# Layer 0 of a four-layer graph network: per-node weights generated on TensorE, 128 nodes at a time, and applied to all eight batches

## The chip, the cores and the metric

The kernel runs on one core of one Trainium2 chip. The time is the device time of one execution in microseconds (us), and lower is better. One core has TensorE for matmuls (PE, with PEld for its weight loads), VectorE (DVE), ScalarE (ACT), GpSimd (POOL) and SyncE (SP, here only a queue that issues transfers). Sixteen DMA engines move the data. PE writes to PSUM, eight banks of 512 f32 values in each of 128 partitions, and DVE or ACT carry the results from there to SBUF.

## What is computed

The input x is 8 batches x 2048 nodes x 64 features in f32, adj is a 2048 x 2048 adjacency matrix whose rows are normalised. Four layers follow each other; each takes the layer norm and relu of x as h, and adds to x what its layer makes of h. The change is in layer 0:

```python
w = jnp.einsum('nd,dkio->nkio', embedding, weight)   # N=2048, D=16, K=3, 64 -> 64
b = jnp.einsum('nd,do->no', embedding, bias)
As = [eye(N), A, 2.0 * (A @ A) - eye(N)]
x_g = jnp.einsum('knm,bmc->bnkc', stack(As), x)      # x is h here
out = jnp.einsum('bnki,nkio->bno', x_g, w) + b
```

So each node has three 64 x 64 weight matrices of its own, a mix of 16 shared ones with the node's embedding as coefficients. Layer 1 takes three steps of adjacency product, two small maps and a relu. Layer 2 is one adjacency product and a map, layer 3 comes down to a sum over all nodes.

## The kernel before, in words

The 8 batches go as 4 pairs p; a pair fills 128 feature rows (2 x 64). The 2048 nodes are 4 blocks nb of 512 columns and 16 chunks m of 128 rows. BT (L94) holds the sign pattern of the adjacency matrix, [128, 16 chunks, 2048], 128 KB in each partition for the whole run; the row scales come back through crow (`load_crow`, L199), a row that is broadcast by a DMA, when a product leaves PSUM (`scaled`, L288). An operand of a product is held as two rounded parts H and L (`halves`, L275), so one block of a product is 32 matmuls 128 x 128 x 512 (`chunks`, L303). A product of all nodes is 4 such blocks.

Layer 0 needs, per pair, t1 = A h and t2 = A t1. The t1 products of pairs 0 and 1 are made in the prologue while the adjacency rows arrive (L593 to L656). The main loop (L858 to L960) then goes pair by pair: for pairs 2 and 3 the four blocks of t1 (`term1`, L488), then for each block its t2 (L923) and `node_weights` (L814). That function makes, for 128 nodes t and 8 embedding indices dg, all 8 mixes' outputs at once on PE: 6 f32 matmuls (3 terms x 2 batches, each on its own half of the array's rows, L828) into the PSUM tile y. DVE then multiplies each of the 8 blocks of 64 columns by that node's embedding value and adds it to x, one scalar_tensor_tensor each (L837). A block of 512 nodes is 48 of these matmuls and 64 of these DVE instructions. Behind each block come layer 1's norm and the storing of x (`keep`, L806).

The first term t0 is h turned to feature rows: `store_planes` (L167) splits h into 16-bit planes and stores them, `load_planes` (L182) reads them back with two transposing DMAs on SP, `join_planes` (L193) puts them together on ACT. `split_next` (L178) and `go_on` (L254) are called between pieces of work and take the next such step, or the next stage of a norm (`norm_stages`, L220). `make_weights` (L689) prepares the small matrices of the later layers. Layer 1's operands are made by `begin_next` (L772) and `first_operand` (L788); its step is `step1` (L1017).

Each engine takes its instructions in a fixed order. The order is settled when the program is built, from the order of the code, the buffers that are free and the `issue_after` marks, so a transfer can stand earlier in its queue than its line suggests, but never goes round another one at run time. MD is a copy of BT's pattern in DRAM in bf16, stored one chunk per block (L951) and read by layer 1's tests of the input (`test_load`, L975).

## Time and profile before

| what | value |
|---|---|
| median of 3 runs | 1176.61 us (1176.37 to 1176.89) |
| the profiled execution | 1180.88 us, of which its span is 1179.2 us |
| PE busy | 1157.1 us (98%) |
| DVE, ACT, POOL busy | 745.2, 293.9, 243.6 us |
| end of the prologue's last product, start of layer 0's main part | 79.15 us |
| first product of layer 1 | 609.44 us |
| DMA | 147 MB, mean 125 GB/s |

A line of a view of groups reads: source line, engine, operation, output <- inputs by the program's names, shapes, count | busy us, mean ns of one | idle time of the engine just before them. The chain of waits is followed back from the last instruction; each piece has its start, its length and what it is. An f32 matmul leaves two records in these views, so `x96` are 48 matmuls; a matmul on the rounded parts leaves one.

### The profile page before, as it was taken

The numbers are of one execution on the slowest core, as the hardware profiler recorded it, in microseconds if no ns is written. First come the engines' busy times: TensorE is split into PE (matmuls) and PEld (weight loads), VectorE is DVE, ScalarE is ACT, GpSimd is POOL, SyncE is SP. The second block draws the span as 40 slices with busy tenths as digits, with TensorE's granted clock in tenths as the row PEclk, the third lists the DMA queues.
The fourth block names the chain that finished last, engine by engine and source line by source line (L and its number), as shares of the span: only waits on it lengthen the run. The fifth ranks groups of instructions, "written<-read, shape, count | busy, mean of one in ns | idle before, by whom it ended". The sixth has DMA issues, their size and how long they took to land.

```text
span 1179.2 us, 19459 instructions
## 1 busy us (share of the span) xinstructions
PE 1157.1 (98%) x7614; PEld 802.6 (68%) x7614; DVE 745.2 (63%) x1933; ACT 293.9 (25%) x465; POOL 243.6 (21%) x259
## 2 busy tenths in 40 slices
PE   9999999999999999999999999999999999999995
PEld 7775555555575556755557777777777777787884
DVE  5557888777847777277775436545643755565674
ACT  5721222111121111111122343334323433211110
POOL 5611332211132111011110004002300410241121
PEclk9999999999999999999999999999999999999998
DMA  9973554323342234222219534663853464441432
GB/s 351 401 191 86 152 151 124 107 74 81 80 140 81 72 84 97 69 56 70 67 54 206 126 82 135 149 137 100 187 118 95 131 160 104 130 152 59 138 114 75
DMA packets 131478, 147.02 MB, mean 125 GB/s; under 512 B 77512, under 2 KB 90312, under 8 KB 129328
## 3 DMA queue, kind: packets, MB, share of 16 engines
q1 hardware_dynamic: 114496, 86.25, 28.8%
q0 software_dynamic: 13456, 53.66, 14.9%
q10 hardware_dynamic: 3424, 5.77, 1.5%
q8 instruction: 62, 1.02, 0.4%
q14 instruction: 40, 0.33, 0.1%
HBM read 88.74 MB, written 39.59 MB: 109 GB/s over the span
## 4 chain that ended last, share of the span: by engine, by line
PE 79%; DVE 7%; DMA 6%; issue 4%; POOL 2%; ACT 1%; POOLq 0%; ACTq 0%; DVEq 0%; SPq 0%
PE bv L306 32%; PE y L828 26%; PE bv_2b L306 3%; PE bv_1b L306 3%; PE bv_3b L306 3%; PE bv_0b L306 2%; PE bn L753 2%; PE ph L1028 2%; DMA acc<-xs 2%; DVE z L227 2%; DMA xs<-acc 2%; POOL rstd L240 1%; DMA BT<-in_adj_dram 1%; PE bv_2a L554 1%; PE bv_1a L554 1%
## 5 line engine op out<-in xcount | busy, mean ns | idle before, releaser
L306 PE MATMUL bv<-BT,H 128*128 128x512 f32 x768 | 302.8, 394 | 0.0
L306 PE MATMUL bv<-BT,L 128*128 128x512 f32 x768 | 299.2, 390 | 0.0
L837 DVE SCALAR_TENSOR_TENSOR acc<-y,emb,acc 128x128 f32<-128x128 f32 x512 | 175.9, 344 | 57.1 <-PE y L828 57.1
L306 PEld LDWEIGHTS bv<-BT,H 128*128 128x128 f32 x768 | 144.1, 188 | 37.2 <-PE bn L753 6.5
L306 PEld LDWEIGHTS bv<-BT,L 128*128 128x128 f32 x768 | 144.2, 188 | 29.2
L837 DVE SCALAR_TENSOR_TENSOR odd<-y,emb,odd 128x128 f32<-128x128 f32 x448 | 153.1, 342 | 0.0
L240 POOL TENSOR_TENSOR rstd<-var,mhalf 128x8 f32<-128x8 f32 x64 | 106.3, 1663 | 173.4 <-DVE var L237 173.0
L828 PE MATMUL y<-wt,t0T 64*128 64x512 f32 x512 | 137.9, 607 | 2.6 <-DVE odd L837 1.6
L306 PE MATMUL bv<-BT,L_u 128*128 128x512 f32 x256 | 101.7, 397 | 3.7 <-DVE L_u L283 3.7
L306 PE MATMUL bv<-BT,H_u 128*128 128x512 f32 x256 | 101.7, 397 | 0.4 <-DVE L_u L283 0.4
L291 DVE TENSOR_TENSOR g<-bv,crow 128x512 f32<-128x512 f32 x48 | 33.1, 689 | 102.2 <-PE bv L306 102.2
L232 ACT ACTIVATE sq<-z 128x512 f32<-128x512 f32 x64 | 40.4, 632 | 202.3 <-DVE z L227 126.3
L828 PEld LDWEIGHTS y<-wt,t0T 64*128 64x128 f32 x512 | 44.1, 185 | 65.7 <-issue 59.6
L809 POOL TENSOR_TENSOR acc<-acc,wl 128x512 f32<-128x512 f32 x16 | 21.4, 1339 | 314.8 <-DVE z L227 314.1
L809 POOL TENSOR_TENSOR acc<-acc,b2r 128x512 f32<-128x512 f32 x16 | 21.3, 1330 | 252.0 <-DVE z L227 252.0
L828 PE MATMUL y<-wt,t1T 64*128 64x512 f32 x256 | 66.8, 589 | 0.0
L243 DVE SCALAR_TENSOR_TENSOR z<-z,rstd 128x512 f32<-128x512 f32 x64 | 43.5, 685 | 35.5 <-POOL rstd L240 35.5
L306 PEld LDWEIGHTS bv<-BT,L_u 128*128 128x128 f32 x256 | 48.6, 190 | 17.1 <-DVE L_u L283 7.2
L173 ACT COPY pl<-z 128x512 uint16<-128x512 uint16 x48 | 27.3, 616 | 130.4 <-DVE z L243 100.2
L306 PEld LDWEIGHTS bv<-BT,H_u 128*128 128x128 f32 x256 | 48.6, 190 | 14.5 <-PE bn_u L753 2.4
L227 DVE SCALAR_TENSOR_TENSOR z<-mean,acc 128x256 f32<-128x256 f32 x112 | 54.8, 532 | 2.6 <-ACT pl L173 2.1
L1034 ACT COPY g<-ph 64x512 f32<-64x512 f32 x64 | 37.2, 581 | 68.9 <-PE ph L1028 67.8
(228 smaller groups left out, 1789.5 us busy)
## 6 DMA issues: line engine op xcount, KB each, us to landing
BT<-in_adj_dram POOLq DMA_DIRECT2D x16, 1024.0 KB, 12.3
crow<-crowD SPq DMA_DIRECT2D x64, 256.0 KB, 3.3
st<-in_adj_dram SPq DMA_DIRECT2D x64, 256.0 KB, 4.0
xs<-acc POOLq DMA_DIRECT2D x32, 256.0 KB, 2.7
MD<-BT POOLq DMA_DIRECT2D x16, 512.0 KB, 5.0
acc<-xs SPq DMA_DIRECT2D x32, 256.0 KB, 4.4
hp<-pl POOLq DMA_DIRECT2D x31, 256.0 KB, 2.6
acc<-in_x_dram SPq DMA_DIRECT2D x24, 256.0 KB, 4.7
```

The lines of the kernel that those rows point to most:

```text
L173: nc.scalar.copy(pl[:, s], hv[:, s])
L227: firsts.append(nc.vector.scalar_tensor_tensor(split(z)[:, :, e], each(mean)[:, :, e, None].to_broadcast([P, 4, C]), -1.0 / C, nodes(xt)[: ...
L232: squares.append(nc.scalar.activation(sq, z, AF.Square))
L240: powers.append(nc.gpsimd.tensor_tensor(rstd, var, mhalf, op=ALU.pow))
L243: scales.append(nc.vector.scalar_tensor_tensor(groups(h), g, 0.0, rstd[:, :, None].to_broadcast([P, 8, C]), op0=ALU.max, op1=ALU.mult))
L291: ahead.append(nc.vector.tensor_tensor(to, ps.rearrange("p (q t) -> p t q", t=4), crow, op=ALU.mult))
L306: nc.tensor.matmul(ps, hl[m // 4][i][:, m % 4, :], BT[:, m, nb * 512:(nb + 1) * 512], start=(m == 0 and i == 0), stop=(m == NCH - 1 and i ...
L554: last = nc.tensor.matmul(ps, hls[p][m // 4][i][:, m % 4, :], BT[:, m, nb * 512:(nb + 1) * 512], start=(m == 0 and i == 0), stop=(m == NCH ...
L809: nc.gpsimd.tensor_tensor(nodes(acc), nodes(acc), more, op=ALU.add)
L828: nc.tensor.matmul(y[:, bb, :], terms[k][hs_, ts], wt[hs_, k, dg * 512:(dg + 1) * 512], start=(k == 0), stop=(k == K - 1),)
L837: last = nc.vector.scalar_tensor_tensor(xj, yd, ec, old, op0=ALU.mult, op1=ALU.add)
L1034: nc.scalar.copy(gT[nb + i][two[bb], :], ph[bb][two[bb ^ i], :])
```

## The change

All of layer 0's products come first, for all four pairs, and then one stage makes and applies the weights for all eight batches.

**Products.** After the prologue six rounds run, each four blocks of 32 matmuls: t2 of pairs 0 and 1, then t1 and t2 of pair 2 and of pair 3. Each block's result, t1 and t2, is stored to DRAM (TD) by `store_t`, two DMAs on SP with runs of 64 values; t0 takes the same way as soon as it is joined. Behind the first 8 blocks run the norms of pairs 2 and 3, behind the next 8 the planes of pairs 0 and 1; `add_bias` adds the bias to x on POOL and stores it for 16 blocks. MD is stored in the first 16 blocks. `make_emb` turns the embedding so that its 16 values stand in four groups of rows (0, 32, 64, 96), and `make_wg` loads the 16 shared matrices in that layout and combines the terms, which was done in wt before.

**Weights.** Then BT's chunks 4 to 15 are given up: their space takes w1 and w2, two buffers each, 96 KB per partition. For each of 16 groups of 128 nodes, `make_w` in 6 steps makes the weights with small f32 matmuls (16 rows deep, four row groups), evicted by DVE (half of each step) and ACT (the other half), and `apply_w` multiplies each node's three terms of all 8 batches by that node's weights; nodes n and n + 64 of a group go together, the other one's columns being zeros. The steps of group g + 1 lie between the applications of group g. All these matmuls are chained in the written order. Results go to DRAM (yD).

**After it.** `x1_load` and `x1_add` bring a block's result back, add it to x and start layer 1's norm: for pair 0 between the groups, for pairs 1 to 3 in the steps of layer 1 for the pair before. BT's chunks 4 to 15 are read back from MD by 12 DMAs on POOL that widen bf16 to f32, and layer 1's first operands follow.

The core of the diff:

```diff
-    BT = adjp.tile([P, NCH, N], F32R, name="BT")
+    BTs = [(sums_ if g else adjp).tile([P, 4, N], F32R, name=f"BT_{g}") for g in range(NCH // 4)]
...
+    def store_t(k, p, nb, t):
+        for e in range(2):
+            nc.sync.dma_start(
+                TD[nb][k, :, :, :, 2 * p + e, :].rearrange("i t h q -> i (t h) q"),
+                t[e * C:(e + 1) * C, :].rearrange("i (f q) -> i f q", q=C),
+            )
...
-    def node_weights(p, nb, terms, between):
...
-                y = psums[-1].tile([P, 2, 512], F32, tag="big", name=f"y_{p}_{nb}_{t}_{dg}")
...
-                    last = nc.vector.scalar_tensor_tensor(
-                        xj, yd, ec, old, op0=ALU.mult, op1=ALU.add
-                    )
...
+    rounds = [("b", 0), ("b", 1), ("a", 2), ("b", 2), ("a", 3), ("b", 3)]
...
+            fetch_t0()
+            split_next()
+            if i < 8:
+                norm_0(2 + i // 4, nb)
+            elif i < 16:
+                restage(i // 4 - 2, nb)
+                acc = load_x(0, i // 4 - 2, nb)
+                add_bias(acc, i // 4 - 2, nb)
+            elif i < 20:
+                make_emb(nb)
+            elif i < 22:
+                make_wg(i - 20)
...
+            t = product(hl, nb, nm, term(1 if own else 2, f"t{2 - own}T_{nm}"), crow, fill=fill)
+            store_t(1 if own else 2, p, nb, t)
...
+    def make_w(g, i):
...
+        ps = [psy.tile([P, 2, 512], F32, tag="gen", name=f"gen_{g}_{i}_{h}", bufs=3) for h in range(2)]
+        if i < 4:
+            w, per, at = ws_[g][0], 4, 4 * i
+            for o in range(4):
+                for r in range(4):
+                    rs = slice(32 * r, 32 * r + D)
+                    multiply(ps[r // 2][:, r % 2, o * P:(o + 1) * P],
+                             wg[rs, at + o, :P], e[rs, :], start=True, stop=True)
+        else:
+            w, per, at = ws_[g][1], 8, 8 * (i - 4)
+            for o in range(8):
+                for c in range(2):
+                    for r in range(4):
+                        rs = slice(32 * r, 32 * r + D)
+                        multiply(ps[r // 2][two[c], r % 2, o * C:(o + 1) * C],
+                                 wg[rs, at + o, P:], e[rs, two[c]], start=True, stop=True)
+        for h in range(2):
+            to = w.rearrange("p n (r o) -> p r n o", r=4)[:, 2 * h:2 * h + 2, :, at:at + per]
+            src = ps[h].rearrange("p r (o n) -> p r n o", o=per)
+            moved[h] = (nc.vector.tensor_copy, nc.scalar.copy)[h](to, src)
...
+    def apply_w(g, u):
+        bk, s_ = divmod(u, 8)
...
+        for m in range(3):
+            for j in range(4):
+                x_ = 32 * bk + 8 * j + s_
+                lhsT = (
+                    tt.rearrange("p h b q -> p (h b) q")[:, :, x_], tt[:, 1, :, x_], t2[:, :, x_]
+                )[m]
+                rhs = (w1_[:, x_, :], w1_[:, C + x_, :], w2_[:, x_, :])[m]
+                wide = 32 if m == 0 else 2 * B
+                multiply(yps[g, bk][32 * j:32 * j + wide, s_ * C:(s_ + 1) * C], lhsT, rhs,
+                         start=(m == 0), stop=(m == 2))
...
+    load_group(0)
+    for i in range(6):
+        make_w(0, i)
+    for g in range(NCH):
+        if g + 1 < NCH:
+            load_group(g + 1)
+        u = 0
+        for i, count in enumerate((3, 3, 2, 3, 3, 2)):
+            if g + 1 < NCH:
+                make_w(g + 1, i)
+            for _ in range(count):
+                apply_w(g, u)
+                u += 1
...
+        if g % 4 == 3:
+            x1_load(0, g // 4)
...
+    BTs[1:] = [hi2.tile([P, 4, N], F32R, name=f"BTr_{g}") for g in range(1, NCH // 4)]
+    for m in range(4, NCH):
+        nc.gpsimd.dma_start(bt(m), rows_of(MD, m))
...
+    x1_add()
+    all_done()
+    while splits:
+        split_next()
+    for q in range(3):
+        first_operand(q)
+    begin_next(0, 3)
```

## The prediction

> **What bounds the kernel now.** I read the chain of waits first, then its pieces in order of time, then the groups by form, then stretches of time with their DMA load.
>
> ```profile
> PE 79%; DVE 7%; DMA 6%; issue 4%; POOL 2%; ACT 1%; POOLq 0%; ACTq 0%; DVEq 0%; SPq 0%
> PE bv L306 32%; PE y L828 26%; PE bv_2b L306 3%; PE bv_1b L306 3%; PE bv_3b L306 3%; PE bv_0b L306 2%; PE bn L753 2%; PE ph L1028 2%; DMA acc<-xs 2%; DVE z L227 2%; DMA xs<-acc 2%; POOL rstd L240 1%; DMA BT<-in_adj_dram 1%; PE bv_2a L554 1%; PE bv_1a L554 1%
> ```
>
> TensorE sets the time. A quarter of the chain is y, the matmuls that go. The chain's pieces of pair 1 and of a layer-1 step price them:
>
> ```profile
> 234.28 20.99 PE y L828 x96
> 255.26 7.49 PE bv_2b L306 x32
> ...
> 667.42 1.02 PE ph L1028 x8
> 668.43 0.93 PE bn L753 x64
> 669.37 11.10 PE bv L306 x48
> 680.47 1.09 PE bn L753 x64
> ```
>
> A block of 512 nodes is 7.49 us of product and then 20.99 us of y; 48 f32 matmuls, so one per 437 ns, two of them side by side on the array's halves. Small matmuls pack too: bn is 32 f32 matmuls 64 x 64 x 64 in 0.93 us, one per 29 ns, four at a time.
>
> ```profile
> L837 DVE SCALAR_TENSOR_TENSOR acc<-y,emb,acc 128x128 f32<-128x128 f32 x512 | 175.9, 344 | 57.1 <-PE y L828 57.1
> L1041 DVE TENSOR_TENSOR bn<-bn,wl 128x1024 f32<-128x1024 f32 x16 | 19.7, 1230 | 14.0 <-PE bn L753 14.0
> L424 DVE COPY crow<-pt_c 128x512 f32<-128x512 f32 x4 | 2.8, 691 | 2.2 <-PE pt_c L317 2.1
> L281 ACT CAST H_t<-pt_t 128x512 fp32r<-128x512 f32 x16 | 9.3, 583 | 54.3 <-PE pt_t L317 54.3
> ```
>
> DVE's 1024 small adds wait for PE, not the reverse: they go without gain by themselves. The three other rows price an eviction from PSUM: a COPY of 512 costs what other DVE operations of 512 do, so 1024 cost 1.23 us; on ACT about 1.17 us.
>
> ```profile
> 79.20:609.40 530.20, 527.11 (x2395) 305.08 (x2393) 384.89 (x1227) 88.33 (x146) 103.75 (x110) 1.00 0.34 93
> 30.00:60.00 30.00, 29.79 (x127) 23.13 (x126) 16.46 (x44) 21.66 (x26) 19.29 (x22) 1.00 1.07 395
> 58.00:64.00 6.00, 6.00 (x28) 4.50 (x27) 2.94 (x19) 2.01 (x2) 1.13 (x2) 1.00 1.06 216
> 609.00:716.00 107.00, 106.62 (x880) 83.50 (x880) 53.68 (x102) 36.89 (x62) 12.53 (x17) 1.00 0.58 136
> ```
>
> The columns are the stretch, its length, busy time of PE, PEld, DVE, ACT and POOL, granted clock, DMA share, GB/s. Layer 0's main part lasts 530 us with the DMA engines a third busy. Full, they moved 395 GB/s of long rows while the adjacency came in, and 216 GB/s where the shared weights came in runs of 256 bytes (58 to 64 us).
>
> **The change, part by part.** Against the 530 us:
>
> *Removed: y.* 16 blocks x 20.99 = 336 us of PE. The 24 product blocks stay at 7.49 us, so do the transposes of t1.
>
> *Added: generation and application.* Per group of 128 nodes there are 4 steps of 16 generation matmuls (16 rows x 128 columns, 128 moving), 2 steps of 64 (64 columns, 64 moving) and 16 x 12 = 192 application matmuls (32 or 16 columns, 64 moving).
> A matmul of the first kind streams a quarter of y's 512 columns, and four row groups run where y has two: 437/4/2 = 55 ns, or 109 ns if only two run at once. A step is 0.87 us (to 1.75).
> The second kind has the size of bn: 29 ns, or half if eight tiles run at once; a step is 1.86 us (0.93 to 1.86).
> Application goes in four column groups of 64 moving columns: I take bn's 29 ns, 12 of them 0.35 us.
>
> The matmuls alone would be 4 x 0.87 + 2 x 1.86 + 5.6 = 12.8 us per group. But PSUM decides: a step needs two tiles of three. Its second tile is the one that DVE evicts from the step before, and the order is written, so PE stands there. From the end of a step's generation to its next use: about 0.17 us until the last record has drained, 0.07 to DVE, 1.23 copy, 0.05 back: 1.52 us. In this time PE has 2 or 3 applications, 0.70 to 1.04 us, and two changes of tile size. These cost little: 32 bn matmuls at 437/8/2 = 27.3 ns would be 0.87 us, and the chain shows 0.93 to 1.09, so 0.06 to 0.22 us for both.
> So a group is 4 x (0.87 + 1.52) + 2 x (1.86 + 1.52) = 16.3 us; 16 groups, of which the first has no application beside it, and 5.6 us for the last application: **267 us**. Below, if evictions hide behind applications (loop 1.13 us) and eight tiles run at once: 4 x 2.0 + 2 x 2.06 = 12.1, in all 199. Above, with two row groups and an eviction 24% longer, as ACT's scattered 16-bit copies are (765 ns at L196 against 616 at L173): 4 x 3.57 + 2 x 3.68 = 21.6, in all 352. I take the middle: y already runs its row groups side by side, and nothing in the code lets PE round the eviction.
>
> [...]
> [...]
>
> *Moved: the transfers of layer 0, into the product stage.* For blocks 3 to 15 one block carries the x load, h, the kept x, planes out and in, crow, bias and MD (about 2 MB) and two stores of 256 KB in 256-byte runs plus the transposing reads (0.77 MB). At 395 and 216 GB/s that is 5.1 to 6.1 + 3.6 us, so 8.7 to 9.7 us per block where PE needs 7.49 and some 0.4 for transposes. SP issues two transposes and about seven more:
>
> ```profile
> 88.87 2.53 SPq L186 DMA_TRANSPOSE pt<-hp  x2
> ...
> 114.42 0.38 SPq L156 DMA_DIRECT2D acc<-in_x_dram  x1
> ```
>
> That is 5.1 us, under a block. The new wait on SP: `store_t` stands until `scaled` is done, and behind it stand the next x, planes and crow. Cover: crow has two buffers, lands in 3.3 us and is wanted a block later. If the engines stay full the cover is gone, scaled comes late and PE stops at the second PSUM bank. 13 blocks x 0 to 1.8 us is up to 23; with queueing I bound it by 0 and 40 and take **15 us**. Turning the embedding adds four sets of transposes at 0.44 us: 2 us.
>
> *Added: two joints.* Between products and weights the first embedding load waits for the space of the last product's tiles, then lands (2.3 us, like bn's load) and the first generation starts: **5 us** (3 to 9). What POOL zeroes there is 8 x 0.54 us beside it.
> After the last application layer 1 needs BT's chunks 4 to 15 and pair 0's last block:
>
> ```profile
> BT<-in_adj_dram POOLq DMA_DIRECT2D x16, 1024.0 KB, 12.3
> xs<-acc POOLq DMA_DIRECT2D x32, 256.0 KB, 2.7
> acc<-xs SPq DMA_DIRECT2D x32, 256.0 KB, 4.4
> hp<-pl POOLq DMA_DIRECT2D x31, 256.0 KB, 2.6
> pt<-hp SPq DMA_TRANSPOSE x62, 2.7
> ```
>
> The reload writes 12 MB: 32 us at 395 GB/s, of which the part in group 14's buffer can start 6 us early, so it ends 27 us behind. Pair 0's block goes eviction 0.9, store 2.7, load 4.4, add 0.7, norm 5, planes 1.3, their store, which I put behind the reload in POOL's queue (to 28), reads 5.2, join 1.5, matmuls 1.1, halves 1.4: 37 us. POOL's norm power and the kept x stand behind the twelve issues (12 x 0.57 us), inside this chain. PE has the first operands (3.3), two half products (7.4), the map (1.0) and four chunks (1.9), 13.6 us of work meanwhile: **24 us** of standing. Below, with only the reload binding, 27 - 13.6 = 13; above, with 2 us more on each of five transfers, 34.
>
> *Moved into layer 1:* 12 adds and norms of pairs 1 to 3, 0.7 + 4.2 us of DVE each, 59 us over six steps of 33.4 us. DVE is half busy there (53.7 of 107), so it fits; in front of a `scaled` it can hold PE: **6 us** (0 to 15).
>
> **Sum:** -336 + 267 + 2 + 15 + 5 + 24 + 6 = -17 us. The profiled execution, 1180.9, would become 1164; its median stands 0.4% lower, and 1176.6 - 17 = **1160 us**.
>
> **The rivals.**
> *A, evictions and generation hide* (199 instead of 267): 1092 us. For it: bn's row shows small tiles near their best rate. Against it: the three PSUM tiles. 0.14.
> *B, slower: four row groups don't run side by side.* Generation at 109 ns gives 4 x 3.27 + 2 x 3.38 = 19.8 us per group, 322 in all, so +38: 1215 us. It decides above 55 + 17/1024 us = 71 ns per matmul. For it: every matmul here uses at most two row groups. 0.18.
> *C, slower: the transfers set the pace of the products.* At 11 us a block, 13 blocks cost 40 instead of 15 and the last planes come late at the first joint (+10 more): 1195 us; it decides above +32 us in that stage. For it: the sum of bytes above; against: half of these stores are wanted only by later groups. 0.18.
> *D, slower: the strided stationary columns load slowly.* At L1173 a load of 32 columns passes every 18 ns (16 in 0.38 us, less one's length); if strided ones took four times that, like 128 columns, an application would be about 1.2 us, a loop 3.3 instead of 1.52, over 96 steps +171 us: 1331. It decides from a loop of 1.7 us. 0.08.
>
> **How the numbers follow.** My case, 1160, has 0.42, with its own bounds 1120 to 1190. Faster by over 0.2%, about what a measurement of this kernel can tell from no change: A's 0.14, most of mine (0.36), a little of C: 0.52. Within: 0.05. Slower: B, C, D and the tail of mine, 0.43. The terms' extremes give 1057 to 1293; leaving out 2 in 10, 1100 to 1245.
>
> **What would show it.** Right: 16 groups of about 16 us with PE idle some 0.5 us per step behind the DVE copy; products of 8 to 9 us; a gap of 20 to 30 us before layer 1's second half products. Wrong: generation matmuls spaced by over 71 ns, applications that fill the loop, DMA full and PE idle between products, or layer-1 steps over 34 us.

## The result, and the profile after

The changed kernel takes 1426.91 us (median of 4 runs, 1426.03 to 1430.72), the kernel before 1176.75 us on the same chips: a ratio of 1.213 (95% interval 1.210 to 1.215), 250 us slower. Its profiled execution is 1426.7 us, the span 1425.0.

The page of the changed kernel, its slices, the queue that brings in instructions (packets, MB, share), and the chain of waits by engine and by line:

```profile
PE   6975768779699999999997479998898999999996
...
PEclk8997888899755555555556679999999999999998
DMA  9998868886611122222223956639738737443332
...
q8 instruction: 146, 2.39, 0.7%
...
PE 54%; DMA 13%; issue 13%; SPq 7%; POOL 6%; DVE 5%; ACT 2%; POOLq 0%; DVEq 0%; ACTq 0%
PE bv L321 19%; PE gen L990 14%; PE yb L990 12%; SPq L353 3%; DMA hp<-pl 2%; POOL rstd L254 2%; SPq L199 2%; POOL acc L813 1%; PE bn L757 1%; DMA crow_0b<-crowD 1%; PE bv_0a L560 1%; PE bv_1a L560 1%; PE bv_2a L560 1%; DMA yt<-yD 1%; DVE z L257 1%
```

Before, the chain was PE 79%; now it is 54%, and issue has gone from 4% to 13%, the DMA engines from 6% to 13%, SP's queue from 0% to 7%. In slices 12 to 21 TensorE is busy nine tenths or more, but its granted clock there reads 5 tenths (0.55 between 420 and 600 us). The mean granted clock over the span is 0.995 before and 0.818 after. The instruction queue moved 62 packets before and 146 now.

The groups of the weights stage (busy us, mean ns of one, idle before):

```profile
L990 PE MATMUL gen<-E,wg 16*64 16x64 f32 (+1 forms) x6144 | 214.9, 349 | 28.5 <-issue 13.0
...
L1023 DVE COPY w<-gen 128x1024 f32<-128x1024 f32 x96 | 117.6, 1225 | 262.5 <-PE gen L990 260.7
...
L1023 ACT COPY w<-gen 128x1024 f32<-128x1024 f32 x96 | 97.2, 1012 | 304.4 <-PE gen L990 304.4
...
L990 PE MATMUL yb<-w,tt 128*16 128x64 f32 (+1 forms) x4096 | 162.6, 303 | 9.5 <-issue 9.2
```

The evictions last what was predicted, and both engines wait for TensorE some 260 to 300 us. TensorE waits for them in the first generation alone, 4.8 us in all:

```profile
383.85 2.09 PE L990 MATMUL gen<-E,wg 16*128 16x128 f32 x32 [0.89 <-DVE w L1023]
386.86 2.09 PE L990 MATMUL gen<-E,wg 16*128 16x128 f32 x32 [0.92 <-DVE w L1023]
```

Stretches of the span, columns as in the prediction (busy time of PE, PEld, DVE, ACT, POOL; granted clock; DMA share; GB/s):

```profile
60.00:90.00 30.00, 30.00 (x145) 23.41 (x144) 16.40 (x52) 9.03 (x12) 9.99 (x17) 1.00 1.07 264
90.00:125.00 35.00, 12.92 (x48) 10.16 (x47) 0.69 (x1) 0.00 (x0) 4.42 (x9) 0.66 1.01 214
...
160.00:200.00 40.00, 33.05 (x132) 26.95 (x133) 13.61 (x24) 13.35 (x22) 12.79 (x13) 0.88 0.70 176
...
475.00:500.00 25.00, 24.67 (x790) 21.93 (x783) 8.06 (x8) 6.66 (x7) 0.00 (x0) 0.50 0.17 49
794.00:830.00 36.00, 17.74 (x58) 10.78 (x58) 8.40 (x17) 5.69 (x10) 10.12 (x17) 0.63 1.01 312
830.00:870.00 40.00, 32.12 (x191) 24.82 (x190) 17.64 (x35) 8.63 (x15) 6.69 (x8) 0.87 0.61 147
```

The first two lines are the end of the prologue and the start of the products: TensorE full, then 13 of 35 us at a clock of 0.66, with the DMA engines full at 214 GB/s. Between 160 and 200 us it has 33 of 40. In the weights stage it is busy 24.67 of 25 us, at 0.50. The last two are the joint to layer 1.

By stage, from the start of the first matmul of one to that of the next (the last application, 793.6 us, ends the weights):

| stretch | before | predicted | after | off by |
|---|---|---|---|---|
| start to the first t2 product | 79.2 | 79.2 | 90.0 | +11 |
| products, to the first generation | - | 216.3 | 290.5 | +74 |
| weights | - | 267 | 413.1 | +146 |
| layer 1 to the end | 569.8 | 599.8 | 631.4 | +32 |

216.3 is the 530.3 us of the main part less 336, with the 2, 15 and 5 us of the prediction. The four differences make 263 us, and 1426.7 - 1164 is 263.

### The profile page after: what moved, and what is told of

It is laid out like the page before. It is cut to its first block, busy times and chain, and to the rows that moved or that the text cites. A ratio compares the mean times of both kernels' runs of the same rounds, so it can differ in the third digit from the quotient of the medians.

```text
span 1425.0 us, 40912 instructions
## 1 busy us (share of the span) xinstructions
PE 1243.7 (87%) x18378; PEld 1014.0 (71%) x18378; DVE 600.8 (42%) x1025; ACT 401.5 (28%) x584; POOL 292.5 (21%) x335
## 3 DMA queue, kind: packets, MB, share of 16 engines
q0 software_dynamic: 16304, 69.91, 14.8%
## 4 chain that ended last, share of the span: by engine, by line
PE 54%; DMA 13%; issue 13%; SPq 7%; POOL 6%; DVE 5%; ACT 2%; POOLq 0%; DVEq 0%; ACTq 0%
PE bv L321 19%; PE gen L990 14%; PE yb L990 12%; SPq L353 3%; DMA hp<-pl 2%; POOL rstd L254 2%; SPq L199 2%; POOL acc L813 1%; PE bn L757 1%; DMA crow_0b<-crowD 1%; PE bv_0a L560 1%; PE bv_1a L560 1%; PE bv_2a L560 1%; DMA yt<-yD 1%; DVE z L257 1%
## 5 line engine op out<-in xcount | busy, mean ns | idle before, releaser
L990 PE MATMUL gen<-E,wg 16*64 16x64 f32 (+1 forms) x6144 | 214.9, 349 | 28.5 <-issue 13.0
L321 PE MATMUL bv<-BTr,H 128*128 128x512 f32 x576 | 227.7, 395 | 3.5 <-ACT H L296 3.5
L1023 DVE COPY w<-gen 128x1024 f32<-128x1024 f32 x96 | 117.6, 1225 | 262.5 <-PE gen L990 260.7
L321 PE MATMUL bv<-BTr,L 128*128 128x512 f32 x576 | 225.8, 392 | 0.9 <-DVE L L298 0.9
L990 PEld LDWEIGHTS gen<-E,wg 16*64 16x64 f32 (+1 forms) x6144 | 185.1, 234 | 52.4 <-issue 40.7
L990 PE MATMUL yb<-w,tt 128*16 128x64 f32 (+1 forms) x4096 | 162.6, 303 | 9.5 <-issue 9.2
L990 PEld LDWEIGHTS yb<-w,tt 128*16 128x16 f32 (+1 forms) x4096 | 117.5, 151 | 28.8 <-issue 24.2
L990 PE MATMUL yb<-w,t 128*16 128x64 f32 x2048 | 115.6, 301 | 1.1 <-issue 1.0
L813 POOL TENSOR_TENSOR acc<-acc,b2r 128x512 f32<-128x512 f32 x16 | 21.5, 1342 | 388.8 <-DVE z L241 245.9
L321 PE MATMUL bv<-BT,H 128*128 128x512 f32 x192 | 77.8, 405 | 5.4 <-ACT H L296 4.6
L321 PE MATMUL bv<-BT,L 128*128 128x512 f32 x192 | 75.6, 394 | 1.1 <-DVE L L298 1.1
L1160 DVE SCALAR_TENSOR_TENSOR junk<-mt,cols,st 128x512 uint8<-128x512 bf16 x64 | 47.8, 747 | 15.3 <-DMA mt<-MD 14.8
```

The source lines that it names most:

```text
L321: nc.tensor.matmul(ps, hl[m // 4][i][:, m % 4, :], bt(m)[:, nb * 512:(nb + 1) * 512], start=(m == 0 and i == 0), stop=(m == NCH - 1 and i ...
L813: nc.gpsimd.tensor_tensor(nodes(acc), nodes(acc), more, op=ALU.add)
L990: steps_y.append(nc.tensor.matmul(*args, **how))
L1023: moved[h] = (nc.vector.tensor_copy, nc.scalar.copy)[h](to, src)
L1160: nc.vector.scalar_tensor_tensor(junk, mt, cols[:, i, :], st, op0=ALU.mult, op1=ALU.not_equal, accum_out=bad[:, i, q:q + 1],)
```

## The experiments

The diffs are excerpts. All numbers are of one profiled execution where no interval is given; the kernel before took 1176 to 1180 us beside them. Stages that an edit doesn't touch still moved: where the product stage is the changed kernel's, it took 285 to 290 us, and the stretch behind the last application, where that is as in the changed kernel, 626 to 638. The changed kernel's profile has 290.5 and 631.4, so a difference of the whole time is good to some 10 us, and the stage that was edited tells more. A group's time is the pitch between groups: from the first application to the last generation, through 15 groups. It is 24.8 us in the changed kernel.

Theories for the weights stage: **E**, the prediction's, TensorE stands for the eviction; **F**, its instructions don't arrive faster; **C**, the array works at half clock.

### Evict twice

```diff
+            for _ in range(2):
                 moved[h] = (nc.vector.tensor_copy, nc.scalar.copy)[h](to, src)
```

> Each half of a step's weights is copied out of PSUM twice, so DVE has 2.45 us and ACT 2.0 us per step in place of 1.23 and 1.01. Theory E (the prediction's: TensorE stands until the eviction gives its PSUM tile back): the loop of a step grows by about 1.2 us, 96 steps, +118 us, and the idle time of TensorE behind the copy grows by as much. Theories F (instructions arrive too slowly) and C (half clock): both engines have slack, a group stays at 25 to 26.5 us and the time within 15 us of the changed kernel's 1427.

1448.5 us; a group 26.4 us. Its copies on the page:

```profile
L1024 DVE COPY w<-gen 128x1024 f32<-128x1024 f32 x192 | 234.9, 1223 | 164.6 <-PE gen L990 161.9
```

117 us more of copying on DVE cost 21.5 us in all (29 in the weights stage), and DVE still waits 162 us for TensorE. E would have made it 118. Beside applications the eviction had slack; E falls as the limit of the groups. It holds in the first generation, which has no applications beside it: that went from 21.2 to 27.8 us. The groups took 1.6 us more each, not as idle time but at a lower clock, 0.50 against the changed kernel's 0.55; why the clock fell was not tried:

```profile
420.00:600.00 180.00, 175.81 (x5157) 154.80 (x5147) 106.89 (x96) 88.36 (x94) 4.27 (x4) 0.50 0.19 54
```

### Narrow applications, split applications

```diff
+                n_ = 8 if m else C
                 multiply(
-                    yps[g, bk][32 * j:32 * j + wide, s_ * C:(s_ + 1) * C], lhsT, rhs,
+                    yps[g, bk][32 * j:32 * j + wide, s_ * C:s_ * C + n_], lhsT, rhs[:, :n_],
```

> The second and third application matmul of each node (128 of the 192 in a group) take 8 moving columns in place of 64, so the products of the second node's first two terms and of both nodes' third term are left out for 56 of 64 outputs; the number of instructions is the same. Theory C (the array at half clock sets the group, 58 ns for an application of 64 columns): 128 x about 42 ns less, a group goes from 25.6 to about 20 us and the kernel loses about 85 us. Theory F at its mean (a page of 256 instructions every 4.2 us, six pages per group): a group stays at 25 us and the kernel within 15 us of 1427; F at its fastest observed page (3.45 us): a group 20.7 us.

1391.2 us, 36 less; a group 22.9 us. It lies between: C alone wanted 20, F at its mean 25. F's own span went from 20.7 to 25, so this run alone decides nothing. Its stretch from 420 to 600 us, where an f32 matmul counts as two MATMUL in the column of PE and two LDWEIGHTS in that of PEld (the 3072 generation matmuls of the changed kernel are its 6144 `gen` records):

```profile
420.00:600.00 180.00, 163.49 (x6008) 149.12 (x6005) 67.19 (x65) 55.47 (x62) 4.91 (x5) 0.50 0.22 62
```

```diff
+                for c in (range(0, C, C // 2) if m else (0,)):
+                    n_ = C // 2 if m else C
                     multiply(
+                        yps[g, bk][32 * j:32 * j + wide, s_ * C + c:s_ * C + c + n_], lhsT,
+                        rhs[:, c:c + n_], start=(m == 0), stop=(m == 2 and c > 0),
```

> The same 128 matmuls per group are each made as two of 32 moving columns: the moving columns of a group are the same, its instructions go from 1536 to 2048, two more pages of 256. Theory F: 2 x 3.45 to 4.2 us more per group, 7 to 8.4 us, +110 to +134 us. Theory C: the array streams as long as before, so a group grows by under 2 us, under +32 us. Theory E: nothing.

1493.9 us, 67 more; a group 29.4 us. Also between: more than C allows, less than F. Its instruction queue on the page:

```profile
q8 instruction: 178, 2.92, 0.8%
```

The same stretch:

```profile
420.00:600.00 180.00, 148.73 (x6216) 133.98 (x6219) 52.22 (x50) 43.74 (x49) 4.26 (x4) 0.58 0.18 49
```

8192 instructions more brought 32 packets more (178 against 146): 256 instructions in each. In 180 us TensorE took 6216 + 6219 of them, 69 per us. The changed kernel in the same stretch:

```profile
420.00:600.00 180.00, 172.19 (x5586) 152.71 (x5584) 61.41 (x58) 50.82 (x56) 4.25 (x4) 0.55 0.20 58
```

62 per us, at a clock of 0.55. Per group TensorE's busy time is nearly the same in both, 23.7 and 24.3 us (its share of the 180 us times the group); the split kernel's idle time is 5.1 us against 1.1, nearly all put down to issue. So I read the two theories as holding by turns: the half clock holds the changed kernel somewhat below the rate at which instructions can come, and that rate holds the split kernel.

### More rows of the array

```diff
-                    rs = slice(32 * r, 32 * r + D)
+                    rs = slice(32 * r, 32 * r + 32)
```

> The generation matmuls read 32 rows per row group in place of 16; the 16 new rows are zeros in both operands, so the numbers, the instructions and the moving columns are the same and only more of the array is in use. If the clock stays at half because small tiles count as low activity, it rises in this stage and a group falls from 25.6 to at most 22 us (limited then by F), -60 us; if it is halved by the gaps alone, or theory F or E holds, the group stays at 25 to 26 us and the time within 10 us of 1427.

1378.7 us, 48 less; a group 22.2 us. The same stretch:

```profile
420.00:600.00 180.00, 139.06 (x6085) 121.15 (x6079) 69.03 (x69) 56.38 (x63) 6.38 (x7) 0.91 0.22 61
```

The same instructions and moving columns, and the clock is 0.91 in place of 0.55. Rows that hold nothing but zeros are enough, and the clock rose though the gaps grew from 8 to 41 us: it was the use of the array, not the gaps, that kept the clock at half. Only this one step, from 16 to 32 rows, was tried. And now TensorE is busy only 139 of 180 us: 41 us are put down to issue, in stops of up to 2.1 us. The rate is 68 per us, as in the split kernel (69) and the narrow one (67, at a clock of 0.50; that one has little idle time, so the half clock may hold it too). Three kernels with clocks of 0.50, 0.58 and 0.91 and groups of 22 to 29 us meet at the same rate: that is F, and I read it as a ceiling of 67 to 69 instructions per us, or 256 in 3.7 to 3.8 us.

The changed kernel shows the same in one of its few stretches at full clock (1.00 between 421.6 and 429.7 us; start, length, instruction, count, wait before it):

```profile
421.66 0.88 PE L990 MATMUL gen<-E,wg 16*64 16x64 f32 x60 [0.37 <-issue]
422.47 0.46 PE L990 MATMUL yb<-w,tt 128*32 128x64 f32 x16
422.75 0.29 PE L990 MATMUL yb<-w,t 128*16 128x64 f32 x8
422.86 0.41 PE L990 MATMUL yb<-w,tt 128*32 128x64 f32 x16
423.09 0.29 PE L990 MATMUL yb<-w,t 128*16 128x64 f32 x8
423.31 1.08 PE L990 MATMUL gen<-E,wg 16*128 16x128 f32 x19
425.54 0.72 PE L990 MATMUL gen<-E,wg 16*128 16x128 f32 x13 [1.15 <-issue]
...
429.73 0.26 PE L990 MATMUL yb<-w,tt 128*16 128x64 f32 x3 [0.74 <-issue]
```

Sixteen records of `yb` with `tt` and eight with `t` are 12 f32 matmuls: 0.39 us from one application to the next (422.47, 422.86), near the 0.35 of the prediction. But TensorE stands before 421.66, 425.54 and 429.73, some 4 us apart, and the profile names nothing that it waited for. Between the stops it takes instructions far faster: the 60 records of the first line and their loads are 120 instructions in 0.88 us. In this kernel's weights stage, between 400 and 780 us, the packets of the instruction queue start 3.3 to 6.1 us apart, 4.2 on average. So I read it as the coming of the next 256 that holds it, not the rate of taking them. Why they don't come faster was not tried.

### Fewer instructions

```diff
-    wg = l0p.tile([P, D, K * C], F32, name="wg")
+    wg = l0p.tile([P, D, K * C], F32R, name="wg")
...
-        es_[g] = typ.tile([P, P], F32, tag="E", name=f"E_{g}", bufs=2)
+        es_[g] = typ.tile([P, P], F32R, tag="E", name=f"E_{g}", bufs=2)
```

On top of the 32 rows, the 64 generation matmuls of 128 moving columns of a group are in f32r. Each leaves one MATMUL and one LDWEIGHTS where it left two of both: 5120 records of `gen` in place of 6144, and 128 instructions fewer of a group's 1536, half of 256.

> [...] Against the run with 32 rows (1379 us, 22.4 us per group): theory F gives 1.7 to 1.9 us less per group, 27 to 30 us in all; a limit by array time would give 64 x about 50 ns, 3.2 us per group, 51 us; theory E nothing.

1365.3 us, 13 less; a group 20.7 us, 1.5 less. Near F's number per group, and not that of array time. In all it gave half of what it should; the stretch behind the last application got 10 us longer.

```diff
-                for c in range(2):
-                    for r in range(4):
-                        rs = slice(32 * r, 32 * r + D)
-                        multiply(
-                            ps[r // 2][two[c], r % 2, o * C:(o + 1) * C],
-                            wg[rs, at + o, P:], e[rs, two[c]], start=True, stop=True,
-                        )
+                for r in range(4):
+                    rs = slice(32 * r, 32 * r + 32)
+                    multiply(
+                        ps[r // 2][:, r % 2, o * C:(o + 1) * C],
+                        wgp[rs, at + o, :], ep_[g][rs, :], start=True, stop=True,
+                    )
```

> On top of the 32 rows: the third term's weights of nodes n and n + 64 come out of one matmul (32 rows that hold the embedding of both, a block-diagonal stationary operand of 128 columns) in place of two, all f32. 64 matmuls, 256 instructions, one page of six less per group; the columns that the array streams stay the same, since two column halves ran side by side before. Against the run with 32 rows (1379 us, 22.4 us per group): theory F 3.5 to 3.7 us less per group, 52 to 59 us in all; a limit by array time or by eviction: under 8 us.

1352.0 us, 27 less; a group 19.4 us, 2.8 less.

```profile
420.00:600.00 180.00, 158.68 (x5844) 141.20 (x5840) 78.96 (x79) 65.29 (x73) 8.54 (x8) 0.94 0.29 77
```

256 instructions less gave 2.8 us per group, most of F's 3.5. TensorE's busy time per group stayed at 17.1 to 17.2 us; its idle time fell from 5.1 to 2.3. So no array time was taken away. Of the 15 x 2.8 = 42 us, 15 were given back outside the groups: the first application came 5 us later, the stretch behind the last one was 12 us longer, and the last group took 2 us less. Why that stretch grew was not tried.

On top of the pairs, all generation matmuls are in f32r, 2048 records of `gen` in place of 4096.

> [...] A group has 128 f32r and 192 f32 matmuls, 1024 instructions, four pages in place of five. Theory F at the 3.75 us per page that the runs so far agree on: a group 15 us in place of 19.5, the kernel 1352 - 15 x 4.5 = 1285 us. If something else holds the group at 19.5 us, for example the eviction, it stays over 1340. The prediction's own loop (1.52 us of eviction behind each step's generation) would be 6 x 1.52 = 9.1 us plus generation, under 15.

```diff
-    wgp = typ.tile([P, D, P], F32, name="wgp")
+    wgp = typ.tile([P, D, P], F32R, name="wgp")
```

1302.1 us, 50 less; a group 16.3 us.

```profile
420.00:600.00 180.00, 153.64 (x5553) 135.03 (x5549) 92.80 (x90) 77.85 (x87) 41.23 (x63) 0.85 0.37 87
```

62 per us: 26 us of the 180 are idle, nearly all in front of `yb` and put down to issue. F's 15 us would have been 68 per us. This run doesn't tell F from array time: per group the idle time stayed at 2.4 us, and the 3.1 us less are all in TensorE's busy time, from 17.1 to 14.0.

> On top of that: the application matmuls are f32r too, written to partitions 0 to 15 only, so one after the other on the array in place of four column groups side by side, with eight evictions of 16 x 512 per group in place of two of 128 x 512. A group has 320 f32r matmuls, 640 instructions, 2.5 pages: theory F alone 9.4 us. The array now streams 192 x 64 columns one after the other, 5.3 us at the full clock by the 27 ns that 64 columns took and 10.6 at half clock, beside 3 to 4 us of generation; so a group is 9.4 to 14.5 us and the kernel 1200 to 1285 us. If it stays at 15 us or more, instruction supply was not what held the run before.

```diff
-                    yps[g, bk][32 * j:32 * j + wide, s_ * C:(s_ + 1) * C], lhsT, rhs,
+                    yps[g, bj][:2 * B, s_ * C:(s_ + 1) * C], lhsT, rhs,
```

1314.0 us, 12 more; a group 17.6 us. The expectation fails. By its own last sentence the supply was then not what held the run before; that isn't settled, because this kernel has a new limit of its own. Its 640 instructions come at 35 per us, half of the 67 to 69, so they are no longer held by their supply. By the program all its applications stand in one column group, and I take them as following one another: between 475 and 500 us, at a clock of 0.50, 422 records, generation among them, took 24.69 us, 58 ns each, where the changed kernel at that clock had 24 records of applications in 0.64 us, 27 ns each. The mean clock is 0.65, and the evictions wait for the stores of yD (ACT 39 us, DVE 29 us between 410 and 630 us); how these two share the time was not tried.

The weights stage of all these kernels; the fourth column is what a group would take at 3.7 us per 256 instructions. The split kernel and those with 32 rows down to 1408 instructions lie within 0.3 us of it. The pairs lie 0.9 and 1.5 us above it, and what adds that was not tried:

| kernel | instructions per group | group us | at 3.7 us per 256 | clock, 420 to 600 us |
|---|---|---|---|---|
| split | 2048 | 29.4 | 29.6 | 0.58 |
| changed | 1536 | 24.8 | 22.2 | 0.55 |
| narrow | 1536 | 22.9 | 22.2 | 0.50 |
| 32 rows | 1536 | 22.2 | 22.2 | 0.91 |
| 32 rows, f32r for 64 | 1408 | 20.7 | 20.4 | 0.85 |
| pairs | 1280 | 19.4 | 18.5 | 0.94 |
| pairs, f32r generation | 1024 | 16.3 | 14.8 | 0.85 |
| all f32r | 640 | 17.6 | 9.3 | 0.65 |

### The prologue

```diff
-    nc.sync.dma_start(b2r, b2[None, :].to_broadcast([P, C]))
+    with tc.issue_after(td_stores[-1].ins):
+        nc.sync.dma_start(b2r, b2[None, :].to_broadcast([P, C]))
```

> The small loads on SP (b2r and the columns of b1, b2, b_nl, w_nl and the intervention value) stand behind the first stores of t1 in place of ahead of the prologue's loads. If they delay the adjacency's first rows, the prologue ends at 79 to 81 us in place of 89.8 and the kernel loses 8 to 11 us; if the prologue grew for another reason, it stays at 88 to 90 us and the time within 4 us of 1427.

1418.1 us, 8.8 less; the first t2 product starts at 81.0 us in place of 90.0. In the changed kernel SP issues eleven small loads from 1.8 to 13.5 us, which nothing holds back any more; one of them, of w_nl, is in the chain (start, length):

```profile
10.10 10.54 DMA wnl<-in_L_gnn_w_nl_dram
```

The cause of the longer prologue is shown. That the kernel gains by it is not: the first generation starts at 377.2 us, no earlier than in the kernels whose prologue still ends at 88 to 90 us (375 to 381), so the product stage took some 9 us back. The 8.8 us lie in stretches that move by as much without this edit.

### The product stage

Here T blames the small packets of the stores, B the bytes, W single late transfers, M the stores of MD. The expectations' 281 us end with the last product; to the first generation it is 290.5.

```diff
-    TD = [dram.tile([K, C, 4, 2, B, C], F32, name=f"TD{nb}") for nb in range(NB)]
+    TD = [dram.tile([K, C, B, 4, 2, C], F32, name=f"TD{nb}") for nb in range(NB)]
...
-                TD[nb][k, :, :, :, 2 * p + e, :].rearrange("i t h q -> i (t h) q"),
+                TD[nb][k, :, 2 * p + e].rearrange("i t h q -> i (t h q)"),
```

> TD is laid out with the batch outside the nodes, so that a store writes one run of 2 KB per row in place of eight runs of 256 bytes, and the loads of the weights stage read the runs of 256 bytes instead. Theory T (the small packets of the stores hold the DMA engines, SP and so the z tiles in the product stage): the stretch from the first t2 product to the first generation, 281 us in the changed kernel, falls to 230 to 245 us, and the kernel to about 1380 to 1390; the wait of TensorE at the start of that stretch (22 us behind DVE's t1T_3a) goes. Rival (the sheer bytes of MD, x, h and planes): the stretch stays over 265 us. If the 256-byte reads hurt the weights stage instead, a group grows over 26 us there.

1417.4 us; the stage 274.2 us, 16 less than 290.5 (11 to 16 less than the 285 to 290 of the kernels with the same stage), about a third of what T wanted. TensorE's 22 us wait for `t1T_3a` fell to 8. In the records of the packets a run of 256 bytes took 21 ns on its engine and one of 2 KB 121 ns, so long runs move only 1.4 times as much in the same time. DMA share was 0.83 to 0.84 from 125 to 280 us, against 0.70 to 0.89 in the changed kernel. The small packets account for a small part; as the cause of the length T falls.

The next kernels turn h on TensorE and leave out the test of the input:

```diff
-                join_planes(pt, term(0, f"t0T_{p}_{nb}"))
-            store_t(0, p, nb, joined[-1])
+            store_t(0, p, nb, to_feat(pt, term(0, f"t0T_{p}_{nb}"), f"t0_{p}_{nb}"))
```

> h is turned to feature rows by TensorE (four transposes and one copy per block, as the embedding is) from the h that is stored anyway, in layer 0 and in layer 1, in place of 16-bit planes that are stored and read back turned; the test of the input that chooses between the two paths of the program is left out, with its loads and its DVE work in layer 1. So only the product stage and the weights stage can be compared with the changed kernel. In the product stage 16 stores of planes and 8 of the 24 loads go, some 6 MB of 53; TensorE gets 16 x 0.44 = 7 us more. Theory B (bytes set the pace): the stretch from the first t2 product to the first generation goes from 281 to 255 to 275. Rival W (single late waits, among them the chain planes, store, turned read, joining, store of t0): the chain is shorter and it may fall below 255. A group stays at 24.5 to 25.5 us.

The stage 267.0 us, 23.5 less. B's range.

```diff
-        add_bias(acc, p, nb)
...
-        acc = load_x(1, p, nb)
+        acc = load_x(0, p, nb)
```

> On top of that, and with layer 1's sums moved into the weights stage as in the run of 1408 us: the second load of x for pairs 0 and 1, the bias sums and the stores of x for 16 blocks leave the product stage; the bias is added where layer 0's result is added, from x itself. That is 16 x (256 + 128) KB and 8 x 256 KB, 8 MB less of some 47 MB. Theory B: the product stage falls by another 25 to 45 us against the run before it in this call. Rival W: by under 12 us.

249.3 us, 17.7 less: below B's range, above W's. One wait stayed in each of these kernels. TensorE's longest waits in the product stage of the changed kernel (us in total, times, longest):

```profile
PE bv_1b L321 <- DVE t1T_3a L306: 22.1, 1, 22.1
PE pt_t L332 <- DMA t1b<-t1D: 11.8, 2, 8.4
PE bv_0a L321 <- DVE t2T_2b L306: 9.6, 2, 6.9
```

SP's issues there (start, length, count):

```profile
77.56 36.47 SPq L353 DMA_DIRECT2D TD<-t1T  x8
114.08 2.39 SPq L353 DMA_DIRECT2D TD<-t1T_0a  x2
```

And some of POOL's:

```profile
90.69 0.54 POOL L934 DMA_DIRECT2D MD<-BT  x1
...
92.36 1.06 POOL L934 DMA_DIRECT2D MD<-BT  x2 [1.12 <-DMA crowD<-crow]
...
95.06 1.57 POOL L934 DMA_DIRECT2D MD<-BT  x3 [1.64 <-DMA crowD<-crow]
```

`t1T_3a` needs one of three buffers, the z tiles, and a z tile is free once its store has left, `t1T_0a`'s first (DVE waits 29.1 us for that transfer before `t1T_3a`). That store stands at 114 us, behind the eight stores of pair 0's t1, whose issues took SP 36 us. Beside them POOL issues MD: 14 of the 16 stores of 512 KB between 61 and 97 us (the next expectation says 11), six of them after 90. In the kernel before each stood behind that block's store of x, at 116, 145 and 174 us.

```diff
             if i < NCH:
-                nc.gpsimd.dma_start(rows_of(MD, i), btf(i))
+                with tc.issue_after(kept[-1].ins):
+                    nc.gpsimd.dma_start(rows_of(MD, i), btf(i))
```

> On top of the run with h turned on TensorE (1393 us): the store of each of MD's 16 chunks (512 KB) stands behind the store of x of its own block, as it did in the kernel before, in place of wherever POOL's queue is free. In the changed kernel 11 of the 16 are issued between 61 and 97 us, in the kernel before one per 29 us. Theory M (these 8 MB fill the DMA engines from 60 to 120 us, so that the first 12 stores of t1 take up to 8 us each to issue, the z tiles stay taken and TensorE stands 22 us behind t1T_3a, after which the clock is at half for a while): the 22 us wait goes, the stretch from the first t2 product to the first generation falls from 267 to 230 to 245 us and the kernel to 1355 to 1372. Rival B (the sum of bytes counts, not when they go): the same bytes only move later, the stretch stays over 258.

1387.1 us; the stage 267.3 us: nothing gained there. SP's issues now:

```profile
76.95 6.01 SPq L359 DMA_DIRECT2D TD<-t1T  x8
83.01 1.43 SPq L359 DMA_DIRECT2D TD<-t1T_0a  x2
84.53 2.86 SPq L359 DMA_DIRECT2D TD<-t1T_1a  x2
87.49 1.54 SPq L359 DMA_DIRECT2D TD<-t1T_2a  x2
```

TensorE's longest waits:

```profile
PE pt_t L338 <- DMA tl<-hs: 47.3, 8, 11.7
PE gen L992 <- DMA E<-embD: 8.2, 1, 8.2
```

The mechanism is as M says, eight issues in 6 us and no wait for `t1T_3a`. But the wait came back as 47 us for the loads of h, where it had been 28. M falls as a cause of the length.

```diff
-            fill = {12: turn_t0}
+            fill = {12: lambda: (turn_t0(), fetch_t0())}
```

> On top of the spread MD stores (1387 us): the load of h that is to be turned is issued a block before TensorE turns it, in place of half a block; bytes and instructions are the same. In that run TensorE waited 47 us for these loads, between 90 and 240 us alone. Rival W (single late transfers in front of an engine that takes its instructions in order): the wait falls under 15 us, the stretch from the first t2 product to the first generation from 267 to 225 to 240, the kernel to 1345 to 1360. Theory B (the first 16 blocks are paced by the bytes, whichever instruction the wait shows at): the wait moves to another line again and the stretch stays over 255.

1372.4 us; the stage 254.6 us, 12.7 less: just below B's 255, far from W's 240. TensorE's longest waits:

```profile
PE gen L991 <- DMA E<-embD: 8.8, 1, 8.8
PE pt_t L338 <- DVE mean L245: 6.8, 1, 6.8
PE pt_t L338 <- DVE t1T_2a L312: 4.8, 2, 2.5
PE pt_t L338 <- DVE L_t L304: 4.4, 1, 4.4
```

The stretch from 90 to 240 us of the kernel before this edit:

```profile
90.00:240.00 150.00, 102.66 (x422) 82.90 (x422) 40.81 (x70) 15.99 (x28) 55.19 (x63) 0.83 0.88 221
```

And of this one:

```profile
90.00:240.00 150.00, 124.91 (x546) 100.34 (x545) 41.93 (x76) 20.10 (x34) 50.41 (x57) 0.93 0.90 224
```

The wait is gone from the loads (4.0 us are left), and TensorE does 125 us of work where it did 103, its clock up from 0.83 to 0.93. The DMA engines are busy 0.90 of the stretch at 224 GB/s. So order was worth some 13 us, and what is left stands beside engines that are nearly full. 6 and 8 MB less were worth 18 to 24 us and 18. I count the bytes as the main limit of the first 16 blocks, and the order of the transfers as the smaller one; that is a judgement and not shown, and how the last 25 to 40 us over 216 divide was not settled.

### Layer 1

```diff
-        if g % 4 == 3:
-            x1_load(0, g // 4)
+        if g >= 3:
+            x1_load((g - 3) % 4, (g - 3) // 4)
```

> The sums x + layer 0 and layer 1's norms of pairs 1 to 3 for node blocks 0 to 2 move from layer 1's steps into the weights stage, one behind each group, where DVE is busy 9 of 25 us and the DMA engines 0.2; only block 3 of each pair stays in layer 1. If these 12 blocks are what stretches layer 1's steps of pairs 0 and 1 (TensorE idle 9 us at 950 to 1030 and 7 us at 1070 to 1110, DMA share 0.85), layer 1 loses 10 to 15 us and the weights stage gains under 3: 1412 to 1418 us. If layer 1 is longer for another reason, it stays within 4 us of 1427; if the norms get in the way of the evictions, a group grows and the kernel is slower than 1430.

1407.8 us, 19 less, but not for the reason given. From the last application to the end it is 626.5 us in place of 631.4, no less than in some kernels with the old layer 1 (626 to 638). TensorE's idle time in layer 1 after its first 75 us fell from 17.8 to 8.6 us as expected (13 to 15 in two such kernels); that in the first 75 us grew from 26.1 to 37.3. What is gained is in the weights stage, 11 us shorter: 5 in the groups and 6 behind the last generation. Why was not tried.

### All together

> All parts together: 32 rows, pairs and f32r generation (1302 us by themselves), long runs (-9.5), late small loads (-8.8), layer 1's sums in the weights stage (-19), h turned on TensorE, the bias out of the product stage; the test of the input is left out. If the parts are independent: 1302 - 37 = 1265 less what the two runs above show, some 1200 to 1250 us. It stays slower than the kernel before (1177 us) unless the product stage falls under 215 us.

1251.45 us (1248.39 to 1266.56), ratio to before 1.064 (1.056 to 1.072), just over the upper edge of the expected time. The edits are those shown above. The product stage was 254.7 us, longer than the 249.3 without long runs and late loads, though it began 9 us earlier: the parts are not independent.

```diff
-            if i < NCH:
-                nc.gpsimd.dma_start(rows_of(MD, i), btf(i))
+            if i < NCH // 2:
+                with tc.issue_after(stored[-1].ins):
+                    for m in (2 * i, 2 * i + 1):
+                        nc.gpsimd.dma_start(rows_of(MD, m), btf(m))
...
-        nc.sync.dma_start(t, src[p][:, part(nb), :])
+        (nc.sync if lastp else nc.scalar).dma_start(t, src[p][:, part(nb), :])
```

> The combination of 1251 us, with MD's stores two at a time behind the stores of h of the first 8 blocks, and with the loads of h for turning on ACT's queue in place of SP's, where they stood behind the stores (16 us of TensorE's waits). If the waits are what held the product stage, it goes from 255 to 215 to 230 us and the kernel to 1215 to 1230 us, still slower than the kernel before (1177 to 1180). If the bytes were it, the kernel stays over 1242.

1271.5 us (1264.45 to 1275.62): slower. The stage grew to 273 us. The loads of h on ACT's queue were still waited for, 44 us. The expectation was wrong.

The same with SP's queue kept and `fill` as in the run of 1372 us.

> The first combination (1251 us) with MD's stores two at a time in the first 8 blocks and the loads of h a block ahead, on SP. If the waits count, its product stage goes from 255 to 220 to 235 us and the kernel to 1215 to 1235; if the bytes do, it stays at 1245 to 1265. In both cases slower than the kernel before (1178 us).

1240.6 us (1237.94 to 1247.81), ratio 1.053 (1.048 to 1.058); the stage 242.5 us. It lies between the two: the stage is above the 220 to 235 that the waits wanted, the time just below the bytes' 1245. TensorE still waits 19 us for the loads of h. The page:

```profile
PEclk9998889999689687778857999999999999999998
...
q8 instruction: 115, 1.88, 0.6%
```

The clock in the middle is mostly 0.6 to 0.9, and 115 packets of instructions are left of 146. The parts found give 186 us of the 250 back, of which this kernel owes an unmeasured part to the test that it leaves out.

## Why the prediction was wrong, step by step

- **What bounds the kernel, y removed (-336):** right. Nothing of it is left, and a product matmul still takes some 395 ns.
- **Prices of the new matmuls.** Right at full clock, from start to start: application 0.34 to 0.39 us for 12 against 0.35; generation of the first kind 58 ns against 55, far from the 109 ns of two row groups. At half clock such a generation matmul took 108 ns, one of the second kind 31 ns, and 12 applications 0.64 us. Rival B's bound of 71 ns was passed, by the clock and not by row groups. Rival D is wrong: the stationary columns lie 64 values apart in the kernel, and 12 applications with them took those 0.34 to 0.39 us, not its 1.2.
- **The failing step: "The matmuls alone would be ... = 12.8 us per group. But PSUM decides".** The eviction was priced rightly (1.225 us for 1.23) and didn't decide: doubling it cost 21 us, and only the first generation waited for it. Two things stood in place of it. The sum took each matmul at full clock, from rows of windows that read 1.00, and the tiles of 16 rows didn't hold that clock: 2.6 us per group, by the run with 32 rows. And it counted columns, not instructions: 384 f32 matmuls are 1536 instructions, which didn't come faster than 67 to 69 per us: 22.2 us, 5.9 over the predicted 16.3. 15 x 8.5 = 128 us. The last group's applications took 20.1 us for 5.6, with one stop of 4.9 us put down to issue. The first generation took 21 for 16.3: there TensorE does stand for the copies, and the matmuls ran at a clock of 0.50. With these it is 146.
- **Transfers in the product stage (15, bounds 0 and 40):** the mechanism was right in outline and is rival C's; the size was off: 74 us in this stretch, of which this term is the largest part. `scaled` came late and TensorE stopped, as foreseen, but at the longest wait it was for a free z tile and not for crow. The sum used 395 GB/s, a row of loads with long runs, for 2 MB of a block's transfers; between 90 and 320 us this stage's mix moved 176 to 228 GB/s with the engines 0.7 to 1.0 busy. That MD's stores would come in a bunch was not seen: the diff took away the mark that held them, and the code's order was read as that of the queue.
- **The first joint (5):** 9.4 us of waiting for the first embedding load, just over its upper bound.
- **The joint to layer 1 (24, bounds 13 and 34):** right in its idle time, 26 us. Missing was the price behind the gap: from there to the end TensorE has 39 us more idle time than before and 22 us more busy time, at a clock of 0.75 in the first 75 us.
- **Layer 1's steps (6, bounds 0 and 15):** 14.0 us (17.8 of idle time against 3.8 before), near the upper bound.
- **The prologue:** not in the sum, +11 us. The mark that held the small loads on SP went with wt's load.
- **Rival A** (evictions hide) was right about the evictions, the first generation aside, and wrong about the time.

A busy column on the profile's page wasn't the use of the array here: between 475 and 500 us TensorE was busy 24.67 of 25 us in the changed kernel, at a clock of 0.50, and 17.77 of 25 us with zeros in 16 more rows, at 1.00. Nor did the instructions come without stops: these were 0.4 to 1.2 us long and some 4 us apart in the changed kernel where its clock is full, and up to 2.1 us long in the run with 32 rows.

## What to carry to other kernels

Count instructions as well as columns when work is cut into small matmuls: 67 to 69 per us was the ceiling here, and an f32 matmul left four in the records. Fill the array's rows, with zeros if need be, before the clock is taken for granted (it went from 0.55 to 0.91 here with 32 rows for 16), and price each gap twice, once as idle time and once as work at a lower clock behind it (26 us of idle time at the joint to layer 1, and a clock of 0.75 over the 75 us from there). When an edit takes a line away, look at which transfers were ordered behind it: a mark that is lost can move them forward in their queue, as it did 14 of MD's 16 stores, to between 61 and 97 us.

## What the runs showed of the hardware

- TensorE's instructions came at 67 to 69 per us at clocks of 0.50 (narrow), 0.58 (split) and 0.91 (32 rows); in the changed kernel's weights stage the instruction queue's packets, 256 instructions each, started at least 3.3 us apart.
- The granted clock of the changed kernel stayed at 0.50 for 160 us (434.5 to 594.9) with TensorE 95 to 99% busy, half of its matmuls on tiles of 16 rows; with 32 rows in these, 16 of them zeros, it was 0.81 to 1.00 in stretches of 25 us between 400 and 725 us.
- An issue of a store on SP that otherwise took about 0.6 us took 4.6 us on average between 77.6 and 114 us in the changed kernel, while the DMA engines were full (a share of 1.06).
- A packet of 256 bytes took 21 ns of a DMA engine and one of 2 KB 121 ns, one of 4 KB on POOL's queue 170 to 300 ns, by the stretch of the product stage.
